# A fused Mamba, MLP and expert kernel: other priorities for the output norm's chain, earlier transposes, earlier statistics, and GpSimd's state products in front

## The chip, the cores and the metric

The kernel runs on one core of a Trainium2 chip. The metric is the device time of one execution in microseconds (us). Kernel before: 1598.88 us, median of three runs (1598.85 to 1601.64).

In the profile the engines are PE (TensorE, matrix products), PEld (its weight loads), DVE (VectorE), ACT (ScalarE), POOL (GpSimd) and SP (SyncE, which only issues DMAs here).

## The reference, cut to what matters

The input x has 2048 tokens of 512 float32 numbers.

```python
x = x + attn(layernorm(x))           # a Mamba-2 layer and a gated MLP
x = x + experts(layernorm(x))        # 8 experts, the best 2 of each token

def attn(r):
    h = r + mamba2(rmsnorm(r, ln1_w))
    return h + (silu(rmsnorm(h, ln2_w) @ gate_w) * (rmsnorm(h, ln2_w) @ up_w)) @ down_w

def mamba2(x):
    z, xb, B, C, dt = split(x @ in_proj_w)
    xb, B, C = split(silu(causal_conv(concat(xb, B, C))))      # 4 taps
    y = ssd_chunked(xb * dt, dt * A, B, C) + D * xb            # chunks of 128 tokens, a carried state
    y = rmsnorm(y * silu(z), norm_w)                           # the output norm
    return y @ out_proj_w
```

Between two chunks a state is carried: each chunk adds its own contribution to the decayed state, and reads the state before it.

## The kernel before, in words

**Tiling.** Tokens are cut into 16 chunks of 128 (t = 0 to 15). Two chunks form a block (b = 0 to 7; t = 2b and 2b + 1); four chunks form a block of the MLP (fb = 0 to 3). Everything is float32.

**A block b of the Mamba part.** `prepare(b)` makes the layer norm's statistics (`scales`: L144 and L145 give `mv`, L189 and L190 `rboth`), the normed tokens `hn` (L214), their transposes on PE (`transposed`, L196, into `pt`, copied to `hT` with the norm's weight at L200), `rstd` (L139, L140) and the step sizes. `project` makes the convolved channels: products `pm` (L332), a copy to `pre` on ACT (L344), two small copies on GpSimd (`halo`, L345 and L346), eight operations `ca` on DVE (L351, L353), a silu on ACT (L359) into `xb` or `cs`. `gate` makes `pz` on PE and its silu `zs` (L365). `chunk(t)` is a generator; in its order it yields: `ec` times `cs` on GpSimd (L401, for each half gp; it carries the old state's part), the scores `psc` (L406), exponentials (L412), their products `cum` on DVE (L414), `xd` (L420), `py` with the old state (L431) and with the scores (L439), the new state `pst` (L446), `yd` and `y` (L452, L455), the state (L461, L462) and its copies `sdiag` (L467); `xbt` (L381); the squares of y (`sq`, L475 and L476) and their sums on GpSimd (L478); the output product `po` (L483); and then **the output norm's chain**: `pms` on PE (L486), `ry` (square root on ACT L139, reciprocal on DVE L140), `h` from `po` (L493), the residual on GpSimd (L494) and its DMA issued from ACT (L495), the square sum of h (L498), `r2` (L139, L140), h times r2 (L501). Its last part transposes h (L196, copied to `h2T` at L200). That last part is run later, by `finish(ninth)` in `mamba(b)`.

**The MLP.** `feed_forward(fb)` runs 16 steps c. A step has four groups of products into two PSUM banks, `x1` (called `px` in the profile) and `x2` (`py`; the line is L711 for both): copies of `x1` on ACT (L756, L763), additions on DVE (L738, L744, L770), silus (L739, L745), and at the end of a step L775 on DVE, which multiplies by `x1` and thereby empties it for the next step, and L776 on GpSimd. The result goes through `mlp_down` (`pd`, L695; added at L696). In fb = 0, GpSimd makes combinations of the weights (`mg`, L526 and L527; `ms`, L537 and L538), and ACT issues the DMAs that keep them in DRAM (`early`, L539; `late`, L540).

**Order.** The kernel is written in a tile language whose scheduler orders every engine's instructions at compile time, by priority. `tc.high_priority(n)` puts instructions n places in front of where the program text has them. `tc.issue_after(i)` makes an engine's instructions stand behind instruction i. From b = 2 (`BPF`, the first block beside which a feed-forward block runs) PE alone is in a manual schedule: its instructions stand in the order in which the text makes them. In that part `mamba(b)` is a generator whose pieces alternate with groups of `feed_forward` (through `advance`). [...]

**What holds buffers.** `po` and `py` share one PSUM buffer (tag "y" of pool `ps_y`), all transposes and small products share one (tag "tr"), `sq` and `xd` share one SBUF buffer, `h` and `hn` three.

**The places of the change.** The chain stands under `tc.high_priority(SOON)` with SOON = 100. `prepare(b + 1)` is begun in `mamba(b)` during its first chunk, and its statistics are issued after `behind`, which at that time is `xd` of that same chunk t = 2b. The transposes of h are made by this piece of `mamba`, for the chunk before (`ninth`):

```python
                next(pieces)
                next(halves, None)
                yield
                if n % 4 == 0:
                    finish(ninth)
                if more and n < 3:
                    next(coming)
```

Of the kernel before, what the change touches and what calls it, by code (L numbers as in the profile page):

```python
# [23 lines left out]
TB = 256  # L24
NCH = TB // P
NB = T // TB
FB = 512
NFB = T // FB
DFF = 2048
FH = FB // 2  # L30
FC = 128
# [18 lines left out]
def mamba_mlp_moe(ctx, tc, x, w_in, w_out, w_gu, w_down, par, wr, wg, wu, wd, out):  # L50
# [93 lines left out]
        nc.vector.bn_stats(out=st, in_=src)  # L144
        nc.vector.bn_aggr(out=dst, in_=st)  # L145

    AT_ONCE, SOON = 400, 100

    early = const.tile([P, 1], F32, name="early")
    nc.scalar.activation(early, eps, AF.Sqrt)  # L150
# [168 lines left out]
    def finish(steps):  # L319
        while True:  # L320
            try:
                next(steps)
            except StopIteration as end:
                return end.value
# [57 lines left out]
        return xbt  # L382

    xbts = {}
    summed = None

    def chunk(b, j, dt, ncum, dtdec, cd, cum, ec, xb, cs, zs):

        nonlocal summed, behind
        t = b * NCH + j  # L390
        tok = slice(j * P, (j + 1) * P)
        halves = [slice(half * HD, (half + 1) * HD) for half in range(2)]
        sdt = sdiag[t % 2]
        xbt = xbts.pop(t)
        y = zs[:, :, tok]

        for gp in range(2):

            if t:
                with tc.issue_after(summed):  # L400
                    nc.gpsimd.tensor_tensor(ec[:, gp], ec[:, gp], cs[gp][:, :, tok], ALU.mult)  # L401

            psc = ps_sg.tile([P, 2, 4, P], F32, name=f"psc{t}_{gp}", tag="sg")
            for half in range(2):
                rows = halves[half]
                nc.tensor.matmul(psc[:, half], xb[rows, 2 + gp, tok], cs[gp][rows, :, tok], start=True, stop=True)  # L406


            lt = cum[gp].rearrange("p (a i) q -> p a i q", a=2)
            turns = [(half, i, 8 * gp + 4 * half + i) for i in range(4) for half in range(2)]  # L410
            for half, i, h in turns:
                nc.scalar.activation(lt[:, half, i], lt[:, half, i], AF.Exp, bias=ncum[:, j, h : h + 1])  # L412
            for half, i, h in turns:
                nc.vector.scalar_tensor_tensor(  # L414
                    lt[:, half, i], lt[:, half, i], dt[:, j, h : h + 1], psc[:, half, i], ALU.mult, ALU.mult
                )
            if gp == 0 and t < NT - 1:

                xd = wa.tile([P, 4, 4, HD], F32, name=f"xd{t}", tag="xd", bufs=1)
                added = nc.vector.tensor_tensor(  # L420
                    xd, bc(xbt[:, 0], 2, 4),
                    bc(dtdec[:, j, :].rearrange("p (g i) -> p g i", g=4), 3, HD), ALU.mult,
                )
                if t:
                    behind = added.ins
            if gp:
                yield
            py = ps_y.tile([P, 4, P], F32, name=f"py{t}_{gp}", tag="y")
            if t:
                for i in range(4):  # L430
                    nc.tensor.matmul(  # L431
                        py[:, i, :], sdt[:, gp, i, :], ec[:, gp, i, :], start=(i == 0), stop=False,
                        skip_group_check=True,
                    )
            yield
            if gp == 0:
                yield
            for half in range(2):
                nc.tensor.matmul(  # L439
                    py[halves[half]], xbt[:, 0, 2 * gp + half, :], lt[:, half], start=not t, stop=True,  # L440
                    skip_group_check=True,
                )
            if gp == 0 and t < NT - 1:
                pst = ps_tr.tile([P, 2, 4, HD], F32, name=f"pst{t}", tag="tr")
                for g in range(4):
                    nc.tensor.matmul(pst[halves[g % 2], g // 2], xbt[:, 1, g, :], xd[:, g], start=True, stop=True)  # L446


            yd = wa.tile([P, 4, P], F32, name=f"yd{t}_{gp}", tag="y")
            for i in range(4):  # L450
                at = C_D + 4 * gp + i
                nc.vector.scalar_tensor_tensor(  # L452
                    yd[:, i, :], xb[:, gp, tok], params[:, at : at + 1], py[:, i, :], ALU.mult, ALU.add
                )
            nc.vector.tensor_tensor(y[:, 4 * gp : 4 * gp + 4, :], yd, y[:, 4 * gp : 4 * gp + 4, :], ALU.mult)  # L455

        if t < NT - 1:
            new = state
            if t:
                flat = state.rearrange("p g i d -> p (g i) d")  # L460
                nc.gpsimd.tensor_tensor(flat, flat, bc(cd[:, j].rearrange("p g i -> p (g i)"), 2, HD), ALU.mult)  # L461
                nc.vector.tensor_tensor(state, state, pst, ALU.add)  # L462
            else:
                nc.vector.tensor_copy(state, pst)
            nxt = sdiag[(t + 1) % 2]
            for half in range(2):
                nc.scalar.copy(nxt[halves[half], :, :, half * HD : (half + 1) * HD], new[halves[half]])  # L467

        yield
        if t < NT - 1:  # L470
            xbts[t + 1] = turned_x(t + 1, xb if j == 0 else xc[0])

        sq = wa.tile([P, 8, P], F32, name=f"sq{t}", tag="xd", bufs=1)
        with tc.high_priority(AT_ONCE):
            nc.scalar.activation(sq[:, 0:4, :], y[:, 0:4, :], AF.Square)  # L475
            nc.scalar.activation(sq[:, 4:8, :], y[:, 4:8, :], AF.Square)  # L476
            for n in (4, 2, 1):
                summed = nc.gpsimd.tensor_tensor(sq[:, 0:n, :], sq[:, 0:n, :], sq[:, n : 2 * n, :], ALU.add).ins  # L478
        yield

        po = ps_y.tile([P, D], F32, name=f"po{t}", tag="y")
        for m in range(8):
            nc.tensor.matmul(po, y[:, m, :], w_o[:, m, :], start=(m == 0), stop=(m == 7))  # L483
        yield
        pms = ps_tr.tile([P, 1], F32, name=f"pms{t}", tag="tr")
        nc.tensor.matmul(pms, sq[:, 0, :], ones[:, 0:1], start=True, stop=True)  # L486

        with tc.high_priority(SOON):
            ry = wa.tile([P, 1], F32, name=f"ry{t}", tag="ry")
            rsqrt_eps(ry, pms, scale=1.0 / DI)  # L490
            h = wa.tile([P, D], F32, name=f"h{t}", tag="tok", bufs=3)
            nc.vector.tensor_scalar(h, res[t], mv[:, t, 0:1], rstd[:, t : t + 1], ALU.subtract, ALU.mult)
            nc.vector.scalar_tensor_tensor(h, po, ry, h, ALU.mult, ALU.add)  # L493
            nc.gpsimd.tensor_tensor(res[t], res[t], h, ALU.add)  # L494
            nc.scalar.dma_start(out=resd[t], in_=res[t])  # L495

            m2 = wa.tile([P, 1], F32, name=f"m2{t}", tag="m2")
            nc.scalar.activation(sq[:, 4:8, :].rearrange("p a q -> p (a q)"), h, AF.Square, accum_out=m2)  # L498
            r2 = wa.tile([P, 1], F32, name=f"r2{t}", tag="r2")
            rsqrt_eps(r2, m2, scale=1.0 / D)  # L500
            nc.vector.tensor_scalar_mul(h, h, r2)  # L501
        yield
        fb, off = divmod(t * P, FB)
        if off == 0:
            h2T[fb] = (wk if fb % 2 else wa).tile([P, 2, NK, FH], F32, name=f"h2T{fb}", tag="h2T", bufs=1)
        half, off = divmod(off, FH)
        transposed(h, h2T[fb][:, half, :, off : off + P], params[:, C_L2 : C_L2 + NK])
# [313 lines left out]
    def mamba(b):  # L821
# [12 lines left out]
        for j in range(NCH):  # L834
            pieces = chunk(b, j, dt, ncum, dtdec, cd, *near[j], xb, cs, zs)
            for _ in range(4):

                if n < 2:
                    halves = (gate(b, pair, hT, zs) for pair in (2 * n, 2 * n + 1))
                elif more:  # L840
                    halves = project(b + 1, n - 2, next_hT, *xc)
                else:
                    halves = iter(())
                next(pieces)
                if more and n == 0:
                    next(coming)
                if more and n == 3:
                    next(coming)
                if b == 0:
                    weigh(1)  # L850
                yield
                next(pieces)
                next(halves, None)
                yield
                if n % 4 == 0:
                    finish(ninth)
                if more and n < 3:
                    next(coming)
                elif more and n == 3:
                    ready = finish(coming)  # L860
                next(halves, None)
                if b == 0:
                    weigh(2)
                yield
                if more and n == 0:
                    next_hT = next(coming)
                yield
                n += 1
# [3 lines left out]
            if more:  # L872
                near[j] = spread(b + 1, j, ready[-1])

    BPF = FB // TB
    ninth = iter(())
    flow = []
    tail = iter(())
# [310 lines left out]
```

## Time and profile before

| | |
|---|---|
| median of three runs | 1598.88 us |
| the profiled execution | 1597.42 us |
| its span, first to last instruction | 1595.7 us |
| mean granted TensorE clock | 0.989 |
| PE busy | 1543.7 us |
| DVE busy | 770.5 us |
| ACT busy | 741.4 us |
| POOL busy | 399.9 us |

The profile is of one execution on the chip. A line of the timeline gives the start in us from the span's beginning, the duration, the engine, the line of the kernel, the operation, output and inputs, sizes, the number of instructions, and in square brackets the idle time of the engine before it and who ended it. The releaser is inferred from semaphores, and can be another one that used the same semaphore. A product in float32 is recorded twice, so "x4" of `px` is a group of two. Line numbers are those of the kernel before. Times by stage in the profile: the Mamba blocks alone up to about 214 us, Mamba beside the MLP from there to about 1093 us (the first group of MLP block 3 starts then), and after it the rest of the MLP and the experts.

### The profile page before, as it was taken

How to read it: one execution, taken by the hardware profiler on the slowest of the kernel's cores; microseconds unless marked ns; L12 is line 12 of the kernel's file. 1: busy time of each engine (PE TensorE's matmuls, PEld its weight loads, DVE VectorE, ACT ScalarE, POOL GpSimd, SP SyncE). 2: the span in 40 equal slices, each digit the busy share in tenths (PEclk: the TensorE clock that was granted, in tenths of full speed). 3: DMA queues.
4: the chain of work that ended last, by engine and by line, in shares of the span. 5: the costliest groups of instructions: out<-in, count | busy, mean ns of one | idle time of the engine just before them, and what ended most of it. 6: DMA issues, size and time to landing. Idle time of an engine off the chain costs nothing. (4 is left out here: it accounts for less than half of the span.)

```text
span 1595.7 us, 19155 instructions
## 1 busy us (share of the span) xinstructions
PE 1543.7 (97%) x6308; PEld 1051.4 (66%) x6308; DVE 770.5 (48%) x2018; ACT 741.4 (46%) x1335; POOL 399.9 (25%) x510
## 2 busy tenths in 40 slices
PE   9999888999999999999999999999999999999997
PEld 7556566767666777767676677666777666665563
DVE  7586854554455554645564654434354452221221
ACT  6788776666563775547645543222211221111110
POOL 2533324423242212111212111111011122333331
PEclk9899999999999999999999999999999999999999
DMA  9344434544553543334444522227777333333332
GB/s 316 117 128 136 154 110 162 182 142 147 170 192 132 190 155 113 127 125 138 129 142 160 175 93 86 92 99 265 256 228 228 103 68 58 67 66 67 66 67 33
DMA packets 127456, 218.68 MB, mean 137 GB/s; under 512 B 11584, under 2 KB 71488, under 8 KB 127360
## 3 DMA queue, kind: packets, MB, share of 16 engines
q1 hardware_dynamic: 105088, 166.08, 32.5%
q0 software_dynamic: 8736, 20.45, 7.0%
q10 hardware_dynamic: 13536, 30.94, 5.4%
q8 instruction: 52, 0.85, 0.2%
q14 instruction: 44, 0.36, 0.1%
HBM read 176.01 MB, written 41.42 MB: 136 GB/s over the span
## 5 line engine op out<-in xcount | busy, mean ns | idle before, releaser
L695 PE MATMUL pd<-md,a 128*128 128x512 f32 x512 | 238.5, 593 | 0.0
L332 PE MATMUL pm<-hT,wi 128*128 128x256 f32 x768 | 183.3, 384 | 1.3 <-DVE r L696 0.9
L696 DVE TENSOR_TENSOR r<-r,pd 128x512 f32<-128x512 f32 x128 | 87.6, 684 | 149.1 <-PE pd L695 148.0
L332 PEld LDWEIGHTS pm<-hT,wi 128*128 128x128 f32 x768 | 140.7, 190 | 26.2 <-issue 8.8
L695 PEld LDWEIGHTS pd<-md,a 128*128 128x128 f32 x512 | 97.0, 190 | 74.7 <-issue 66.5
L353 DVE SCALAR_TENSOR_TENSOR ca<-pre,params,ca 128x256 f32<-128x256 f32 x288 | 141.2, 543 | 0.3
L711 PE MATMUL py<-h2T,ms 128*128 128x256 f32 x512 | 132.1, 380 | 0.9 <-ACT up L750 0.7
L776 POOL TENSOR_TENSOR a<-a,up 128x256 f32<-128x256 f32 x64 | 47.8, 748 | 315.1 <-DVE up L770 246.1
L332 PE MATMUL pz<-hT,wi 128*128 128x256 f32 x512 | 123.3, 394 | 0.6 <-DMA wi<-in_w_in 0.6
L1045 PE MATMUL epg<-ew,xgT 128*128 x312 | 118.1, 460 | 0.4 <-issue 0.2
L1045 PE MATMUL epu<-ew,xgT 128*128 x312 | 117.8, 459 | 0.0
L483 PE MATMUL po<-w_o,zs 128*128 128x512 f32 x256 | 112.9, 592 | 0.0
L332 PEld LDWEIGHTS pz<-hT,wi 128*128 128x128 f32 x512 | 98.9, 198 | 19.8 <-issue 4.6
L1066 PE MATMUL epd<-ew,ehT 128*128 (+1 forms) x234 | 107.1, 593 | 1.0 <-DVE ehT L1059 1.0
L412 ACT ACT_TABLE_LOAD x71 | 91.1, 1283 | 34.3 <-DVE ncum L280 28.8
L711 PEld LDWEIGHTS py<-h2T,ms 128*128 128x128 f32 x512 | 95.0, 190 | 18.0 <-DVE a L744 2.4
L412 ACT ACTIVATE cum<-cum,ncum 128x128 f32<-128x128 f32 x256 | 87.1, 394 | 14.7 <-POOL cum L306 12.3
L483 PEld LDWEIGHTS po<-w_o,zs 128*128 128x128 f32 x256 | 48.3, 190 | 55.5 <-issue 54.0
L1026 POOL DMA_INDIRECT xg<-xnd,idx x39 | 38.8, 994 | 176.0 <-PE pt L196 174.0
L1045 PEld LDWEIGHTS epu<-ew,xgT 128*128 128x128 f32 x312 | 59.3, 190 | 33.0
L1072 POOL DMA_INDIRECT out<-ey,idx x39 | 61.9, 1587 | 66.8 <-DVE ey L1071 40.8
L711 PE MATMUL px<-h2T,mg 128*128 128x256 f32 x256 | 68.0, 388 | 10.7 <-DVE a L775 9.9
(248 smaller groups left out, 2504.5 us busy)
## 6 DMA issues: line engine op xcount, KB each, us to landing
wi<-in_w_in SPq DMA_DIRECT2D x80, 512.0 KB, 3.7
ms<-late SPq DMA_DIRECT2D x48, 512.0 KB, 3.7
mg<-early SPq DMA_DIRECT2D x48, 384.0 KB, 3.0
md<-in_w_down SPq DMA_DIRECT2D x64, 256.0 KB, 4.0
cum<-rowsd SPq DMA_DIRECT2D x32, 512.0 KB, 4.6
late<-ms ACTq DMA_DIRECT2D x16, 512.0 KB, 3.1
ec<-rowsd SPq DMA_DIRECT2D x60, 128.0 KB, 3.8
xnd<-xn ACTq DMA_DIRECT2D x28, 256.0 KB, 3.7
```

Source lines behind the costliest of these rows:

```text
L332: nc.tensor.matmul(pm[:, m, :], w[:, k, m * P : (m + 1) * P], hT[:, k, :], start=(k == 0), stop=(k == NK - 1))
L353: nc.vector.scalar_tensor_tensor(ca, pre[:, m, k : k + TB], cw[:, k : k + 1], ca, ALU.mult, ALU.add)
L412: nc.scalar.activation(lt[:, half, i], lt[:, half, i], AF.Exp, bias=ncum[:, j, h : h + 1])
L483: nc.tensor.matmul(po, y[:, m, :], w_o[:, m, :], start=(m == 0), stop=(m == 7))
L695: nc.tensor.matmul(pd, a[:, j * P : (j + 1) * P], d, start=(m == 0), stop=(m == 1))
L696: nc.vector.tensor_tensor(rows[j], rows[j], pd, ALU.add)
L711: nc.tensor.matmul(ps, w[:, k], m[:, k], start=(first and k == 0), stop=(k == KH - 1), skip_group_check=True)
L776: nc.gpsimd.tensor_tensor(a[:, 1], a[:, 1], up, ALU.mult)
L1026: nc.gpsimd.indirect_dma_start(out=xg, out_offset=None, in_=src, in_offset=bass.IndirectOffsetOnAxis(ap=idx[:, n : n + 1], axis=0))
L1045: nc.tensor.matmul(ps, xT[:, k, :], w[:, lo : lo + EI], start=(k == 0), stop=(k == NK - 1))
L1066: nc.tensor.matmul(pd, hT[:n, m, :], w[:n, NG + m * D : NG + (m + 1) * D], start=(m == 0), stop=(m == len(ET) - 1))
L1072: nc.gpsimd.indirect_dma_start(out=out, out_offset=bass.IndirectOffsetOnAxis(ap=idx[:, n : n + 1], axis=0), in_=y, in_offset=None, compute ...
```

## The change

Five edits, in the core of the diff:

```diff
-    AT_ONCE, SOON = 400, 100
+    AT_ONCE = 400
...
+    newest_xd = None
...
             if t:
-                with tc.issue_after(summed):
+                with tc.issue_after(summed), tc.high_priority(AT_ONCE):
                     nc.gpsimd.tensor_tensor(ec[:, gp], ec[:, gp], cs[gp][:, :, tok], ALU.mult)
...
-                if t:
-                    behind = added.ins
+                behind, newest_xd = newest_xd or behind, added.ins
...
-        with tc.high_priority(SOON):
+        with tc.high_priority(AT_ONCE if t == BPF * NCH - 1 else 0):
             ry = wa.tile([P, 1], F32, name=f"ry{t}", tag="ry")
             rsqrt_eps(ry, pms, scale=1.0 / DI)
...
                 next(pieces)
+                if n % 4 == 0 and (b != BPF or n):
+                    finish(ninth)
                 next(halves, None)
                 yield
-                if n % 4 == 0:
+                if b == BPF and n == 0:
                     finish(ninth)
```

- The chain of the output norm has a priority of 400 at t = 3 (`BPF * NCH - 1`), and none at the other fifteen chunks, where it had 100 at all sixteen.
- The transposes of h are made one piece sooner in the text, ahead of half a projection (`halves`) and of one group of the MLP, at every turn but b = 2, n = 0 (the chunk t = 3).
- The statistics of a block are issued behind `xd` of the chunk before the one that they stood behind.
- GpSimd's product `ec` times `cs` has a priority of 400.
- No instruction is computed with other operands than before; nothing is added to or left out of the computation.

## The prediction, on record before the result was known

> **What bounds the kernel now.** First the page's busy times:
>
> ```profile
> PE 1543.7 (97%) x6308; PEld 1051.4 (66%) x6308; DVE 770.5 (48%) x2018; ACT 741.4 (46%) x1335; POOL 399.9 (25%) x510
> ```
>
> TensorE (PE) is the bound: 97% busy, no other engine over half. From b = 2 on its order is the one written in the program, so a moved instruction elsewhere is worth only what it takes off (or adds to) PE's idle time, plus what a slower PE clock costs. So next the waits of PE, longest first in total (columns: waited for, us in total, times, longest us):
>
> ```profile
> PE px L711 <- DVE a L775: 9.9, 7, 1.8
> PE py L431 <- POOL halo L346: 7.5, 2, 5.0
> PE pt L196 <- DVE hn L214: 4.8, 2, 3.7
> PE pt L196 <- DVE h2T L200: 3.1, 4, 0.8
> ...
> PE pt L196 <- DVE mv L145: 1.5, 1, 1.5
> ```
>
> These five are 26.8 us, and all lie in the stages that the change touches. The timeline of PE around the largest (start us, duration us, last the idle time before it):
>
> ```profile
> 195.21 2.05 PE L431 MATMUL py<-ec,sdiag 128*128 128x128 f32 x8 [4.98 <-POOL halo L346]
> ...
> 203.27 0.63 PE L196 MATMUL pt<-ident,h 128*128 128x128 f32 x4 [1.51 <-DVE mv L145]
> 207.63 1.09 PE L196 MATMUL pt<-ident,hn 128*128 128x128 f32 x4 [3.73 <-DVE hn L214]
> 208.51 5.79 PE L332 MATMUL pz<-hT,wi 128*128 128x256 f32 x16
> ```
>
> The first releaser is misnamed. GpSimd's product `ec` (L401) had ended at 188.47, its `halo` copy at 194.73; but `py` shares its only buffer (tag "y") with `po`, and DVE's L493, which empties `po`, ended at 195.11, 0.10 before PE went on. At 117.36 it is the same (L493 ends 117.26). So these two stalls wait for the output norm's chain, not for GpSimd. And sixteen pz records take 5.79 us here against 3.6 us at 347.8. The table of windows tells why (PE busy, PEld, DVE, ACT, POOL, then PEclk):
>
> ```profile
> 117.30:120.70 3.40, 3.34 (x12) 3.10 (x13) 3.40 (x8) 2.61 (x6) 1.30 (x1) 0.50 0.21 80
> 195.20:199.20 4.00, 3.99 (x14) 3.55 (x15) 4.00 (x9) 3.20 (x6) 1.30 (x1) 0.50 0.42 164
> 206.10:212.90 6.80, 5.27 (x15) 4.40 (x16) 4.34 (x7) 4.55 (x7) 2.51 (x2) 0.50 0.01 2
> ```
>
> [...] the granted clock is 0.50 after each of the long waits. [...] L353 took 0.98 each at 185.8 (2.95 for 3) beside a busy GpSimd, 0.41 at 196.6 (2.45 for 6) beside an idle one. [...]
>
> **The change, part by part**, in the built order of each engine.
>
> *A. t = 3: its norm in front, the statistics of b = 3 a chunk sooner.* Before, ACT stood from 189.30 to 192.45 behind two DMA issues (`early`, `late`, released by GpSimd's 192.06), then loaded a table and made `ry` at 194.01. After, the load, `rboth` and `ry` come ahead of those issues: 189.3 + 1.28 + 0.3 + 0.3 = 191.2. But DVE now has six operations on `ca_10`, `ca_11` ahead of its reciprocal of `ry`, beside GpSimd's five products: from 188.9, four at 0.98, two at 0.5 give 193.8; the reciprocal 0.16, one more `ca` 0.5 to 1.0, L493 0.74: 195.2 to 195.8. So the 4.98 us gap stays, or grows by up to 0.6; I take 0.6. Only if the `ca` operations ran at 0.41 would L493 end near 193.0. Then: `cum` x8 2.2, `hn` 0.55, `xd` 1.2, `hn` 0.55, r and h 0.8: h is there at about 201.9, while PE reaches its transposes at 195.8 + 2.0 + 4.7 = 202.5: the 1.51 goes. `hn` is ready, so the 3.73 goes; next late is the single "tr" buffer, 0.78 as at t = 5. Hence `pt<-hn` starts at 202.5 + 0.6 + 0.8 = 203.9 instead of 207.6: 3.7. With no long gap, the half clock of 206.1 to 212.9 doesn't come: its 5.3 busy us shrink by half, 2.6. Sum 6.3; bounds 2.5 (contended throughout) and 9 (the first gap shrinks to 3 as well).
>
> *B. t = 1, the same turn at 117.36.* `ry` comes 1.4 sooner on ACT (one load less ahead), but six `ca` operations (two at 0.37, four at 0.5: 2.8) again precede it on DVE: 112.5 + 2.8 + 0.16 + 0.5 + 0.74 = 116.7 against 117.26. Gain 0.3 after what the transposes lose; bounds -1.5 and 2.2 (a half-clock window more or less).
>
> *C. The chain's priority goes from 100 to 0 for t other than 3.* At t = 4 to 7, PE waits for `a` L775, which empties `x1`. Timeline of ACT, then of DVE, at t = 4:
>
> ```profile
> 266.40 1.28 ACT L139 ACT_TABLE_LOAD   x1
> ...
> 268.01 1.28 ACT L739 ACT_TABLE_LOAD   x1
> 269.30 0.42 ACT L739 ACTIVATE a<-a 128x256 f32<-128x256 f32 x1
> ```
> ```profile
> 270.30 0.49 DVE L501 TENSOR_SCALAR h<-h,r 128x512 f32<-128x512 f32 x1
> 270.70 0.41 DVE L775 TENSOR_TENSOR a<-a,px 128x256 f32<-128x256 f32 x1
> ```
>
> The norm's square root (two loads and 0.3) stands ahead of the silu, and its scaling ahead of L775. After, silu comes first: 266.40 + 0.42 = 266.8 with no load; L775 comes right behind `xd` (ends 267.71), 268.1; `pd` keeps PE busy until 269.39. So the whole gap goes, and likewise at 340.40, 422.64 and 491.74: 1.78 + 1.76 + 1.78 + 1.62 = 6.9. Bounds 5 and 6.9. What is later is h: at t = 4 271.4 instead of 270.8.
>
> *D. Transposes a piece sooner.* At t = 5, 7, 9, 11 `pt<-h` is directly followed by `pt<-hn`, one buffer, 4 x 0.78 = 3.1 waiting for `h2T`. After, 8 pz, 2 px, 2 py lie between (12 products of two records, 24 x 0.216 = 5.2 us): 3.1 goes. The cover: h was ready 11 to 15 us before its transposes at t = 4 to 13, and 5.7 to 9.8 before their new place, so the 0.6 of part C is hidden. At t = 12 `pt<-h` now follows `pt<-xn` and waits some 0.65 for ACT's copy (ends 881.13), but that covers the 0.87 that `pm` waited there: +0.2. At t = 14 it moves by six matmuls, over 4 us of slack left.
>
> *E. GpSimd's products for the state in front.* They end no stall. What they push back: at c = 5 and 13 of the first feed-forward block, `ec` (L401) now precedes `ms` (L538). In the timeline of GpSimd, then of ACT:
>
> ```profile
> 315.03 0.72 POOL L538 TENSOR_TENSOR ms<-ms,mg 128x256 f32<-128x256 f32 x1
> 315.71 1.27 POOL L401 TENSOR_TENSOR ec<-ec,cs 128x512 f32<-128x512 f32 x1
> ```
> ```profile
> 315.79 0.33 ACTq L540 DMA_DIRECT2D late<-ms  x1
> 316.14 1.28 ACT L739 ACT_TABLE_LOAD   x1 [1.06 <-POOL ms L538]
> ```
> ACT's issue of `late` waits for `ms`; the silu's load and silu queue behind it; L775 (ends 318.30) behind the silu; PE's next `px` started at 318.36, 0.06 later, so with no slack (469.77 and 469.82 at c = 13). A 1.27 us product in front becomes a new PE wait of 1.27, twice: -2.5. Bounds -2.6 and 0. At c = 1 the same swap (one add of `sq`, 1.2) holds `xbt` about 0.5, and PE waits for it at 243.40: -0.5. Moved statistics put `rboth` and two `hn` before L775 at c = 3 and 11: 285.8 against 286.8 wanted, hidden by 1.0. SP's moved loads (four, `wi` and `x`) meet no PE wait.
>
> Sum: 6.3 + 0.3 + 6.9 + 3.1 + 0.2 - 2.5 - 0.5 = 13.8. The profiled execution took 1597.42 (span 1595.7 and 1.7 around it): 1583.6. The median shown, 1598.88, is 1.46 above it: 1585.1. I say 1585.
>
> **Rivals.** (1) A gives nothing beyond its idle time, or less: [...] B loses 1.5, and hidden steps of c = 3 and 11 surface at 1 us each: 13.8 - 3.8 - 1.8 - 2 = 6.2, about 1592.7. For it: the first gap stays, and 2.12 us of waiting at 45.3 already brought 10.2 us at 0.50. (2) Slower: the chain without priority misses its earlier transposes, in which case PE, in order, waits at each of ten of them (t = 4 to 13). To end 3.2 above before it must eat 13.8 + 3.2 = 17, so 1.7 at each, h late by 7.4 to 11.5: 1602. Against it: part C's 0.6. (3) Nothing moves: what looks like PE's gain is taken by the next of its waits (248.28, 1.70; 234.01, 0.51, both left alone) and by `late` more often than twice: within 0.2% (3.2 us), 1597.
>
> **Numbers.** Forecast (gain 7 to 20) 0.80, rival 1 0.10, rival 2 0.05, rival 3 0.05. 0.2%, 3.2 us, is about what a measurement of this kernel tells from no change. Faster 0.90, same 0.05, slower 0.05. Range: A at 9 (+2.7), B at 2.2 (+1.9) and no loss at c = 1 (+0.5) make 18.9, with 1 for the spread of the runs 1579; A at 2.5 (-3.8), B at -1.5 (-1.8), C at 5 (-1.9) and 0.5 more in E leave 5.8, so 1593, beyond which lie rivals 2 and 3 and an edge of the others.
>
> **What would show it.** Right: no wait of `px` for `a` at t = 4 to 7; none of `pt` for `h2T` at t = 5 to 11, and one of 0.8 at t = 3; none for `hn`; the half clock after 206 gone; two new waits of 1.2 to 1.3 for L775's line at c = 5 and 13; the gap ahead of `py` at t = 3 still 4 to 6. Wrong: PE waiting for `h` at an early transpose, or a first gap under 3.

## The result, and the profile after

| | before | after |
|---|---|---|
| median | 1598.87 us (4 runs, 1598.45 to 1601.64) | 1587.80 us (4 runs, 1586.32 to 1587.97) |
| the profiled execution | 1597.42 us | 1587.97 us |
| its span | 1595.7 us | 1586.0 us |

The ratio is 0.9925, with a 95% interval from 0.9908 to 0.9942: faster by 11.1 us in the medians and by 9.4 in the profiled executions, against 13.8 forecast. The time is 2.8 above the number that was forecast and inside its range (1579 to 1593). Line numbers of the kernel after are one to three higher than before (L711 is now L713, L775 is L777, L431 is L432, L144 is L145).

The page's busy times after; PE is busy for 0.7 us less, so 9.0 of the 9.7 us that the span lost are idle time of PE:

```profile
PE 1543.0 (97%) x6308; PEld 1051.8 (66%) x6308; DVE 768.4 (48%) x2018; ACT 722.7 (46%) x1321; POOL 403.7 (25%) x510
```

The longest waits of PE after (waited for, us in total, times, longest us):

```profile
PE py L432 <- issue: 6.8, 2, 5.4
PE px L713 <- DVE a L777: 6.7, 5, 3.1
PE pc L269 <- ACT xbt L382: 2.6, 2, 1.4
...
PE pt L197 <- DVE h2T L201: 0.8, 1, 0.8
```

The waits for `hn` and for `mv` are gone from the top, those for `h2T` fell from four to one. But the wait of `px` for L777 fell by only 3.2 us, and its longest is now 3.1 where none was over 1.8. The timeline of PE around t = 3 is as the prediction has it: the first gap is still there (0.4 longer), no wait for `hn`, 0.79 for the buffer:

```profile
197.93 2.04 PE L432 MATMUL py<-ec,sdiag 128*128 128x128 f32 x8 [5.37 <-issue]
199.77 5.43 PE L333 MATMUL pz<-hT,wi 128*128 128x256 f32 x16
205.03 0.60 PE L197 MATMUL pt<-ident,h 128*128 128x128 f32 x4
206.42 0.66 PE L197 MATMUL pt<-ident,hn 128*128 128x128 f32 x4 [0.79 <-DVE h2T L201]
206.91 3.40 PE L333 MATMUL pz<-hT,wi 128*128 128x256 f32 x15
```

The table of windows (after the stretch: PE busy, PEld, DVE, ACT, POOL, then PEclk) shows that the half clock after 206 is gone, and that a new stretch has come at 719:

```profile
206.10:212.90 6.80, 6.48 (x34) 5.46 (x36) 4.53 (x9) 4.47 (x6) 2.77 (x2) 1.00 0.87 291
718.90:722.10 3.20, 3.20 (x8) 2.57 (x9) 3.20 (x11) 0.95 (x3) 0.19 (x1) 0.50 0.00 0
```

What happened at 719? First PE's timeline, then DVE's, of the kernel after:

```profile
714.67 1.16 PE L432 MATMUL py<-ec,sdiag 128*128 128x128 f32 x8
718.90 2.07 PE L713 MATMUL px<-h2T,mg 128*128 128x256 f32 x4 [3.07 <-DVE a L777]
```
```profile
708.63 1.23 DVE L422 TENSOR_TENSOR xd<-xbt,dtdec 128x1024 f32<-128x1024 f32 x1 [1.06 <-ACT sq L500]
709.77 0.69 DVE L145 BATCH_NORM_STATS2 bn<-x 128x6 f32<-128x512 f32 x1
...
712.16 0.49 DVE L503 TENSOR_SCALAR h<-h,r 128x512 f32<-128x512 f32 x1
715.42 0.69 DVE L145 BATCH_NORM_STATS2 bn<-x 128x6 f32<-128x512 f32 x1 [2.77 <-DMA x<-in_x]
716.03 0.17 DVE L290 TENSOR_TENSOR dtdec<-dtdec,dt 128x32 f32<-128x32 f32 x1
716.12 0.68 DVE L698 TENSOR_TENSOR r<-r,pd 128x512 f32<-128x512 f32 x1
716.72 0.61 DVE L352 TENSOR_SCALAR ca<-pre,params 128x256 f32<-128x256 f32 x2
717.25 1.27 DVE L354 SCALAR_TENSOR_TENSOR ca<-pre,params,ca 128x256 f32<-128x256 f32 x3
718.43 0.41 DVE L777 TENSOR_TENSOR a<-a,px 128x256 f32<-128x256 f32 x1
```

The first of the two moved statistics (709.77) finds its tile. The second waits 2.77 us for the load of x15, and everything behind it on DVE waits with it (nothing runs there from 712.65 to 715.42), L777 last. Why does x15 come so late? The pool of x tiles has five buffers, so x15 takes that of x10, and x10 is in use until its residual has been written. In order, from POOL, ACT's queue and SP's queue, and last what SP waited for from 700 to 716 (us, times, longest):

```profile
706.07 1.27 POOL L496 TENSOR_TENSOR x<-x,h 128x512 f32<-128x512 f32 x1 [11.62 <-DVE h L495]
```
```profile
707.37 0.33 ACTq L497 DMA_DIRECT2D resd<-x  x1
```
```profile
711.89 0.33 SPq L79 DMA_DIRECT2D x<-in_x  x1
```
```profile
SPq L79 <- DMA resd<-x: 2.2, 1, 2.2
```

The write is issued at 707.37, SP waits for it, the load is issued at 711.89, and the statistic can start 3.5 later. The answer on the load's line says who waited for it (us in total, times):

```profile
  DVE bn L145: 10.8, 6
```

One of the six is the start of the kernel, which every kernel here has (2.5 to 2.8); the other five, 8.2 us, came with the moved statistics, for b = 2 and 4 to 7.

To see what each costs, the start of the same group of PE was subtracted between two timelines (kernel less before, us; a change between two rows is gained or lost between them):

| PE's start, us in before | before | after | after, again | no_ec | stats_old | bufs6_md3 | b3_exact |
|---|---|---|---|---|---|---|---|
| first `pms`, 76.65 | 0 | 0.4 | 0.1 | 2.2 | 1.5 | 0.9 | -2.2 |
| `psc` of t = 4, 189.10 | 0 | 2.3 | 2.0 | 4.2 | 1.4 | 1.8 | -3.0 |
| first `px`, 214.57 | 0 | -3.8 | -4.6 | -1.8 | 1.6 | -5.0 | -9.7 |
| first `px` of fb = 1, 522.59 | 0 | -11.0 | -12.1 | -11.8 | -5.8 | -6.5 | -17.2 |
| `pst` of t = 10, 666.65 | 0 | -12.3 | -13.4 | -12.6 | -7.1 | -7.8 | -18.4 |
| `px` at 728.71 | 0 | -9.8 | -11.1 | -10.7 | -7.1 | -7.7 | -18.4 |
| `pst` of t = 12, 817.58 | 0 | -9.4 | -10.7 | -10.6 | -8.3 | -9.0 | -19.7 |
| end | 0 | -9.7 | -10.8 | -10.8 | -8.2 | -3.8 | -19.9 |

All these kernels give PE the same instructions between the first rows, though not in the same order. After loses 1.9 us between the first two rows, where among other things the second statistic of b = 2 waits (1.18 at 88.89), and 2.8 between t = 10 and t = 12, where other kernels gain 1.3.

### The profile page after: what moved, and what is told of

Read it like the earlier page. It is cut to its first block, busy times and chain, and to the rows that moved or that the text cites. A ratio compares the mean times of both kernels' runs of the same rounds, so it can differ in the third digit from the quotient of the medians.

```text
span 1586.0 us, 19153 instructions
## 1 busy us (share of the span) xinstructions
PE 1543.0 (97%) x6308; PEld 1051.8 (66%) x6308; DVE 768.4 (48%) x2018; ACT 722.7 (46%) x1321; POOL 403.7 (25%) x510
## 5 line engine op out<-in xcount | busy, mean ns | idle before, releaser
L713 PE MATMUL py<-h2T,ms 128*128 128x256 f32 x512 | 132.1, 380 | 0.9 <-ACT up L752 0.7
L713 PEld LDWEIGHTS py<-h2T,ms 128*128 128x128 f32 x512 | 94.9, 190 | 18.1 <-DVE a L746 2.4
L199 ACT COPY xgT<-pt 128x512 f32<-128x512 f32 x39 | 22.8, 586 | 117.7 <-PE pt L197 117.7
```

The lines of the kernel that those rows point to most:

```text
L713: nc.tensor.matmul(ps, w[:, k], m[:, k], start=(first and k == 0), stop=(k == KH - 1), skip_group_check=True)
```

## The experiments

Theory: A, C and D do what the prediction says, E costs its two waits, and the shortfall is DVE's wait for x tiles. Rival: the shortfall is something else (the priorities, the statistics' own work in a new place, an accident of the clock). The runs were made on three chips, each beside the kernel before, whose medians there were 1599.22 (experiments 1 and 2, stats_b3, and 4), 1597.98 (5, 6 and b3_noec_front) and 1599.21 (b3_exact, front_exact and 8).

**1. GpSimd's product back in its place (no_ec).**

```diff
-                with tc.issue_after(summed), tc.high_priority(AT_ONCE):
+                with tc.issue_after(summed):
                     nc.gpsimd.tensor_tensor(ec[:, gp], ec[:, gp], cs[gp][:, :, tok], ALU.mult)
```

> The changed kernel without its GpSimd edit: the product ec (L403) keeps the planner's place behind ms. Theory (step E): the two new waits of px for L777 at c = 5 and 13 (1.09 and 1.08 us) go and nothing else moves, so 2.2 us below the changed kernel: about 1585.6. Rival (the products in front also bring something, at c = 1 or ahead of py): the waits go, but others of about the same size come back, and the time stays within 0.5 us of 1587.8, or rises.

Measured: 1585.54 us, ratio 0.9910 (0.9896 to 0.9923). In the kernel after, PE waits here at c = 5 (timeline of PE):

```profile
314.13 1.13 PE L713 MATMUL px<-h2T,mg 128*128 128x256 f32 x4 [1.09 <-DVE a L777]
```

and in no_ec the same group starts with no wait:

```profile
312.84 1.88 PE L697 MATMUL pd<-md,a 128*128 128x512 f32 x4
314.57 1.13 PE L713 MATMUL px<-h2T,mg 128*128 128x256 f32 x4
```

Over the first MLP block (rows 3 and 4 of the table) no_ec gains 10.0 where after gains 7.2. So the edit on GpSimd costs 2.8 us and brings nothing that could be seen. By the starts of `px`, each of the two waits costs 1.2; the other 0.3 or so lies around c = 3. The stall at 719 stays (2.53).

**2. Statistics as before (stats_old).**

```diff
-                behind, newest_xd = newest_xd or behind, added.ins
+                if t:
+                    behind = added.ins
```

> The changed kernel with the statistics pinned as before for every b; the other edits stay. Theory: the waits for x tiles go (prologue 2.3, stall at 719 3.8), but at t = 3 the wait for hn (3.73) and the half-clock window after it (2.6) return: 6.1 - 6.3 = about no difference, 1587 to 1589. Rival (the shortfall comes of something else): the loss of A's 6.3 with nothing back, 1594.

Measured: 1589.34 us, 0.9936 (0.9921 to 0.9950). Rows 1 to 2: no loss. Rows 5 to 7: a gain of 1.3 for the loss of 2.8. But between `psc` of t = 4 and the first `px` the gain of 6.1 is gone as well, with the wait for `hn` back (PE's waits):

```profile
PE pt L197 <- DVE hn L215: 4.1, 2, 3.7
```

So the statistics, moved for every b, bring 6.3 and cost 2.0 and 4.1: little on balance (the ratio of 0.9936 is that of the changed kernel within the interval, 0.9925 and in experiment 8 0.9935). What the 2.0 consist of is told under B below.

**3. Statistics sooner for b = 3 alone (stats_b3), and a mend of it (b3_exact).**

```diff
-                behind, newest_xd = newest_xd or behind, added.ins
+                behind, newest_xd = newest_xd if b == BPF else added.ins, added.ins
```

> The changed kernel with the statistics a chunk sooner for b = 3 alone (those that step A needs at t = 3); for every other b they stand where they stood before. Theory (the missed step: the second statistic waits on VectorE for an x tile whose buffer is freed only just ahead): of 10.8 us that VectorE waited for x tiles only the one of b = 3 stays, if any; the loss of 2.3 us ahead of t = 1 and the wait of 3.07 us with its half clock at 719 go, and A's gain stays: 6 us below the changed kernel, 1582 (1581 to 1584). Rival (the shortfall against the forecast comes of something else[...]): within 1 us of 1587.8.

Measured: 1585.08 us, 0.9912 (0.9898 to 0.9926). The waits for x tiles fell to the first (2.7 us, once), the stall at 719 is 0.79. It is above the 1581 to 1584 that were expected. The expectation says too much: at t = 0 the line moves the statistics of b = 1 back by a chunk as well, and the prologue took another order: its first `pms` is 6.0 later than in the kernel before, where after is 0.4 and no_ec 2.2 later. At t = 3 the other order was a gain: the gap ahead of `py` is 0.76, with 3.93 waited later for `h2T`. A mend leaves b = 1 alone:

```diff
+                if t:
+                    behind = newest_xd if b == BPF else added.ins
+                newest_xd = added.ins
```

> The kernel with statistics sooner for b = 3 alone had moved those of b = 1 as well (a chunk later, since at t = 0 nothing may move), and its prologue took 4 us more. Here b = 1 too stands as before, so that against the changed kernel only the statistics of b = 2 and 4 to 7 differ. Theory: from the end of the prologue to t = 2 the loss of 2.1 us against the kernel before falls to 0.3 or less, A stays at -6.1 with its gap of 5.4 ahead of py, and from t = 10 to t = 12 the loss of 2.8 turns into a gain of 1.3 as in the kernels without early statistics there: 5 to 6 below the changed kernel of the same chip, about 1582.5. Rival (the repair before gained from the other order of the prologue and t = 3 alone): 1586 or more.

Measured: 1583.21 us, 0.9906 (0.9892 to 0.9921), 4.8 below the changed kernel on the same chip (1587.97, experiment 8), where each of its runs (to 1584.18) is below each run of that (from 1584.46). Its built order is that of stats_old but for the stage of t = 3. From rows 1 to 2 it gains 0.8, from rows 2 to 3 6.8, from rows 5 to 7 1.3. (Its profile is of its lowest run, 5.5 below its median, so the last row of the table flatters it.) PE and DVE at the place of the stall:

```profile
710.31 1.13 PE L715 MATMUL px<-h2T,mg 128*128 128x256 f32 x4 [0.79 <-DVE a L779]
```
```profile
708.65 1.27 DVE L354 SCALAR_TENSOR_TENSOR ca<-pre,params,ca 128x256 f32<-128x256 f32 x3
709.84 0.41 DVE L779 TENSOR_TENSOR a<-a,px 128x256 f32<-128x256 f32 x1
```

The same group of `px` takes 1.13 us here and 2.07 after: the clock is whole (1.00 in the window 710.30 to 713.50, 0.50 in that after). So the wait for x15 cost 2.3 us of idle time more, and the stretch of about 3.4 us at half clock (an estimate from the clock of wider windows, 0.98 from 715 to 719 and 0.59 from 719 to 723: 4 x 0.02 and 4 x 0.41, over 0.5) some 1.7: together about the 4.1 of rows 5 to 7.

**4. A sixth buffer for x (bufs6_md3).** The statistics stay where the change put them.

```diff
-    xp = pa_stack.enter_context(tc.tile_pool(name="xp", bufs=5))
+    xp = pa_stack.enter_context(tc.tile_pool(name="xp", bufs=6))
...
-        d = pmlp.tile([P, D], F32, name="md", tag="md", bufs=4)
+        d = pmlp.tile([P, D], F32, name="md", tag="md", bufs=3)
```

> The changed kernel with the pool of x tiles at six buffers for five, the room for it taken from the down projection's weights (three buffers for four). Statistics stay a chunk sooner everywhere. Theory (it is the late buffer, not the earlier place of the statistics): VectorE waits for no x tile, and the prologue's loss and the stall at 719 go: 4 to 6 us below the changed kernel, 1582 to 1584, less what later loads of the down weights may cost. Rival (the statistics' own work, 0.6 us for each tile and 0.55 for each hn, stands in VectorE's way in its new place): no wait for x tiles, but the time within 1 us of 1587.8.

Measured: 1593.95 us, 0.9968 (0.9957 to 0.9979): slower than after. The theory's part held and the price of the buffer was far underrated. Waits for x tiles: the first only (2.8). Between the first two rows 0.9 lost instead of 1.9, at 719 nothing, rows 5 to 7 a gain of 1.3. So it is the late tile, not the statistics' own work, that stalls there; of the 1.9 ahead of t = 4 about half is the wait. Against that stand 13 waits for the down projection's weights, which have a buffer less (PE's waits):

```profile
PE pd L697 <- DMA md<-in_w_down: 8.0, 13, 1.6
```

**5. The priority alone (prio_only), the earlier transposes alone (trans_only),** each made in the kernel before:

```diff
-    AT_ONCE, SOON = 400, 100
+    AT_ONCE = 400
+    BPF = FB // TB
...
-        with tc.high_priority(SOON):
+        with tc.high_priority(AT_ONCE if t == BPF * NCH - 1 else 0):
```

> The kernel before with the priority edit alone: the norm's chain in front at t = 3, no priority at all other t. Theory (step C is the priority's alone): the four waits of px for L775's line at t = 4 to 7 (1.78, 1.76, 1.78, 1.62) go, the waits of pt for h2T at t = 5, 7, 9, 11 and for hn at t = 3 stay, no wait for x tiles beyond the one there was: 6.9 below the kernel before, give or take 1 at t = 1 and 3: 1592. Rival (C needs the earlier transposes or statistics too): fewer than two of the four waits go, above 1596.

Measured: 1589.48 us, 0.9955 (0.9943 to 0.9967), 8.5 below before, where 6.9 were expected. The four waits at t = 4 to 7 are gone, the rest is there (PE's waits):

```profile
PE pt L197 <- DVE hn L215: 4.1, 2, 3.7
PE pt L197 <- DVE h2T L201: 3.1, 4, 0.8
PE px L712 <- DVE a L776: 2.9, 3, 1.6
```

Over the first MLP block it gains 8.0, by four steps of 1.9 to 2.0 each.

```diff
                 next(pieces)
+                if n % 4 == 0 and (b != FB // TB or n):
+                    finish(ninth)
                 next(halves, None)
                 yield
-                if n % 4 == 0:
+                if b == FB // TB and n == 0:
                     finish(ninth)
```

> The kernel before with the earlier transposes alone. Theory (step D): the four waits of pt for h2T (0.78 each) go and the four of px for L775's line stay: 3.1 below before, 1596. Rival (with the chain's priority still 100 nothing else moves, but h comes too late for the earlier place): PE waits for h at its transposes, and the time does not fall.

Measured: 1593.33 us, 0.9973 (0.9962 to 0.9983), 4.7 below before, where 3.1 were expected. No wait for `h2T` is left, and the waits of `px` are all there (10.1 us, 7). Between the first `px` and that of fb = 2 it gains 4.3, 1.0 to 1.3 at each of the four places.

**6. Two repairs together (b3_noec):** stats_b3 and no_ec.

> Two repairs of the changed kernel at once: statistics a chunk sooner for b = 3 alone, and the GpSimd product ec in the planner's place as before. Theory: the two add up, since they lie in different stages. From the profile with the statistics alone (end 14.98 us below the kernel before) another 2.3 for the two waits at L777 (1.09 and 1.30 there): a profile 17 below, a median of 1582.5. Rival (the spread of the prologue hides it, or ec in its old place brings another wait back): no lower than 1585.

Measured: 1582.49 us, 0.9908 (0.9894 to 0.9922), as expected, but the medians alone don't show that the two add up: the ratios of stats_b3 and no_ec are 0.9912 and 0.9910, within the interval. Nor is the profile 17 below before, but 14.6, since its first `pms` is 7.8 later. The stages show it: from the first `px` to the end after gains 5.9, no_ec 9.0, stats_b3 9.6 and this one 12.4. What they bring alone, 3.1 and 3.7, is 6.5 together.

**7. And the front at t = 3 (b3_noec_front; with the mend of 3, front_exact).**

```diff
+                with tc.high_priority(AT_ONCE if b == BPF + 1 else 0):
-                nc.vector.tensor_scalar(
-                    hns[j], res[t], mv[:, t, 0:1], rboth[:, t : t + 1], ALU.subtract, ALU.mult
-                )
+                    nc.vector.tensor_scalar(
+                        hns[j], res[t], mv[:, t, 0:1], rboth[:, t : t + 1], ALU.subtract, ALU.mult
+                    )
...
-        transposed(h, h2T[fb][:, half, :, off : off + P], params[:, C_L2 : C_L2 + NK])
+        with tc.high_priority(AT_ONCE if t == BPF * NCH - 1 else 0):
+            transposed(h, h2T[fb][:, half, :, off : off + P], params[:, C_L2 : C_L2 + NK])
```

> The same two repairs, and at t = 3 the transposes' eviction into h2T and the two hn of b = 3 get the front priority as well. With the repaired statistics alone PE waited 3.93 us there for h2T (L201), which stood on VectorE behind eight products of cum, an xd and an hn. Theory: in the built order h2T now stands behind five products of cum and hn is made ahead of the convolution, so the wait falls to about 0.8 (one buffer of tag tr), while the wait of py ahead of it grows by 0 to 0.5: 2.6 to 3.1 below the kernel with two repairs, about 1579.7. Rival (the wait only moves on, to xd or to the next product): no lower than it by more than 1.

Measured: 1579.56 us, 0.9882 (0.9868 to 0.9895). The 2.9 (against b3_noec on the same chip) came, with other parts than expected: the wait for `h2T` is 1.65, that of `py` 1.92, and sixteen records of `pz` take 3.62 us there (5.43 after), so the clock stays whole.

> The kernel with two repairs and the front priority at t = 3, with the statistics of b = 1 back in their place. Theory: the prologue gets its 4 us back, but in the built order the reciprocal of ry stands behind five operations on ca again, so the gap ahead of py at t = 3 is 5.4 and not 1.9, and what follows in that stage is no better: about the same time, 1578 to 1581. Rival (the prologue's length does not depend on that order): 1583.

Measured: 1579.47 us, 0.9884 (0.9867 to 0.9900), as expected: the first `pms` comes 8.1 sooner than in b3_noec_front, but at the first `px` only 0.3 of it is left. 3.1 are lost between, and 4.7 at t = 3, where the gap ahead of `py` is 5.37 again. Both are about 8.3 us below the changed kernel, and beat both kernels; they cannot be told apart.

**8. The changed kernel again (after_again).**

> The changed kernel itself once more, beside the two others on one chip. Theory: 1587.8 within 1.5; the waits for x tiles at about the same places and sizes (10.8 in all), PE's wait of some 3 us at 719 again, while the waits before 80 us differ from run to run[...]. Rival (the stall at 719 was of that one execution): no wait over 1 us there.

Measured: 1587.97 us, 0.9935 (0.9919 to 0.9951). Waits for x tiles 10.4 us, 6 times; the stall at 719 is 2.93. It belongs to the kernel.

## Why the prediction was right or wrong

Measured by the table of starts, each part in the run named; "t = 12" is what was forecast under D for the transposes there.

| step | forecast | measured | from |
|---|---|---|---|
| A, t = 3 | 6.3 | 6.1 | after, rows 2 to 3 |
| B, t = 1, and the rest of rows 1 to 2 | 0.3 | -1.9 | after, rows 1 to 2 |
| C, priority | 6.9 | 8.0 | prio_only |
| D, transposes | 3.1 | 4.3 | trans_only |
| t = 12 | 0.2 | 0.2 | trans_only |
| E, GpSimd in front | -3.0 | -2.8 | no_ec against after |
| second statistics wait at t = 10 and 11 | 0 | -4.1 | after against b3_exact |

The measured parts add up to 9.8, against 9.7 of the span. That the number came so close was in part luck: B and the last row took 6.3 more than forecast, and C and D gave 2.3 more, for which the prediction had no reason. B's -1.9 and C's 8.0 lie outside the bounds that were given for them.

**A** came as worked out: the 4.98 became 5.37 (forecast 5.58), the wait of 0.79 for the buffer took the place of 3.73, and the second half clock went (1.00 from 206.10 to 212.90). That the priority at t = 3 doesn't bring A by itself is shown by stats_old and prio_only, both with 3.73 for `hn`; whether the earlier statistics would bring it without the priority, no run shows. (The prediction's sum for h being there gives 201.1, not 201.9, which changes nothing, since PE was expected at 202.5.)

**C** and **D** were right in place and count, and short in size by 0.2 to 0.5 us a wait. The idle time that the records showed was not the whole cost: waits of 1.62 to 1.78 cost 1.9 to 2.0 (prio_only), waits of 0.78 cost 1.0 to 1.3 (trans_only). Where PE didn't wait, the records of two groups overlapped by 0.15 to 0.2 us (in the kernel after `pz` starts at 199.77 while `py` lasts to 199.97; in no_ec `px` starts at 314.57 while `pd` lasts to 314.72); after a wait that overlap is missing (in the kernel after `px` starts at 314.13, 1.09 behind the end of `pd` at 313.04). By the author's estimate this accounts for about 0.2 of each; the rest of D's is open.

**E** was right: two waits of 1.09 and 1.08 (forecast 1.27). By the starts they cost 1.24 and 1.22. The 0.5 at c = 1 didn't show: the wait for `xbt` grew from 0.57 to 1.45, and the next one of `px` fell from 1.70 to 0.92, but in no_ec they are 1.40 and 0.91 as well, so this isn't the work of the edit on GpSimd.

**B**'s own stage gained more than forecast. Its gap shrank from 2.49 to 1.46, and no half clock follows it (1.00 from 116 to 128): between the starts at 112.25 and 122.12 of before, after gains 2.7. Two losses outweigh this. Ahead of it, from 76.65 to 112.25, the late x tile delays PE by 1.6 (0.3 in bufs6_md3). Behind it, from 122.12 to 144.99, the four profiled kernels with the statistics of all blocks moved (after, after_again, no_ec, bufs6_md3) lose 2.7 each, where stats_old, prio_only and b3_exact lose 0 to 0.7 (stats_b3 loses 3.4, by waits of PE, 2.09 for `dA` the longest). This loss is in no term of the prediction. It comes of PE's order, which is the scheduler's before b = 2, and which changed with the statistics. PE's timeline of before, then of after:

```profile
126.11 1.08 PE L439 MATMUL py<-cum,xbt 128*64 128x512 f32 x4
127.11 1.13 PE L406 MATMUL psc<-cs,xb 64*128 64x512 f32 x4
```
```profile
125.89 1.07 PE L440 MATMUL py<-cum,xbt 128*64 128x512 f32 x2
126.89 0.66 PE L197 MATMUL pt<-ident,hn 128*128 128x128 f32 x4
127.48 1.07 PE L440 MATMUL py<-cum,xbt 128*64 128x512 f32 x2
128.48 1.12 PE L408 MATMUL psc<-cs,xb 64*128 64x512 f32 x2
129.53 1.08 PE L447 MATMUL pst<-xd,xbt 128*64 128x256 f32 x8
130.55 1.12 PE L408 MATMUL psc<-cs,xb 64*128 64x512 f32 x2
```

Four records in a row take as long as two (1.13 and 1.12 for `psc`, 1.08 and 1.07 for `py`): in before two records of `psc` run at once (both in the window 127.10 to 127.60), in after one (128.48 to 128.95). With the transposes of `hn` and with `pst` between them the pairs take 1.07 and 1.12 each, one after the other: about 1.0 lost twice. The other 0.7 is a longer wait for `dA` (0.94 at 147.01, for 0.25).

The stall at t = 10 isn't in the sum either. The other step that failed is one sentence under E: "Moved statistics put `rboth` and two `hn` before L775 at c = 3 and 11: 285.8 against 286.8 wanted, hidden by 1.0. SP's moved loads (four, `wi` and `x`) meet no PE wait." It counted the time of the moved instructions in the first MLP block, and took their input for granted. What it left out is when that input can be there: the second x tile of block b takes the buffer of chunk 2b - 4, whose residual is written at the beginning of chunk 2b - 3. The statistics stood behind `xd` of chunk 2b - 2; now they stand behind that of 2b - 3, and the tile lands 1 to 3 us after they could start. The waits of b = 4, 5 and 6 (1.83, 1.24, 1.17 on DVE) cost PE nothing that the table shows, so part of the sentence held. Those of b = 2 and 7 surfaced: for b = 2 as about 1.0 (the 1.9 of after less the 0.9 of bufs6_md3), for b = 7 as 4.1. In fb = 1 the statement was never tried.

**The rivals.** Rival 1 named the right kind of thing (hidden steps that surface), at the wrong places and 4.9 too slow. The slower rival didn't come: after t = 3 no transposes of `h` wait but those of t = 12, 0.68 us for ACT's copy (0.65 forecast), where `pm` no longer waits its 0.87. And not every loss was needed: with the statistics moved for b = 3 alone, and without the edit on GpSimd, the change is worth 15.5 us (b3_noec, which also has b = 1 a chunk later), and 18 to 20 with the front at t = 3.

## What to carry to other kernels

When a consumer moves forward, look for its inputs before its costs: for each buffer it reads, follow the pool back to who frees it, and compare the landing of the load in the trace of before with the new place. Here one early statistic became a wait for all that stood behind it on DVE (2.77 us at 715.42, and through L777 3.07 on PE); so move such an instruction only where the early place is needed (here one block of seven), and leave the others. And where a scheduler makes the order, compare the order of the bottleneck engine as well: here it parted products whose records had run two at a time, at about 1.0 us for each of the two pairs.

## What the runs showed of the hardware that was not expected

**A half clock may cost little.** In the kernels before and after, a wait of about 2.1 us at 45 (2.12 and 2.15) was followed by some 10 us at half clock (0.50 from 45.60 to 55.90 in before, and from 46.40 to 56.40 in after; a wider window of after: PE busy, PEld, DVE, ACT, POOL, PEclk):

```profile
48.00:58.00 10.00, 10.00 (x29) 6.11 (x28) 3.17 (x10) 5.60 (x13) 7.51 (x6) 0.57 0.11 39
```

In no_ec, with the same built order on PE, the clock stayed whole (1.00 from 44 to 66), and PE then waited instead (timeline of PE):

```profile
68.70 0.38 PE L269 MATMUL pc<-tri,dA 128*32 128x128 f32 x2 [4.81 <-DVE dA L266]
```

At the first `pms` it was 1.8 later than after. In this execution PE at whole clock arrived early and waited for DVE. Not every run is like that: b3_exact had the whole clock as well (1.00 from 44 to 66), waited 1.58 there, and was 2.6 sooner than after. So these runs show no cost of that stretch beyond the spread of the prologue, and not that it has none. That its cost hangs on whether the other engines wait for PE there is the author's guess, and no run tests it.

**Which wait is followed by the half clock isn't told by its length.** Behind waits of 1.96 (prio_only) and 2.15 us (after) at 45 the clock was 0.52 and 0.57 from 48 to 58; waits of 1.82 to 2.17 there in four others (b3_exact, no_ec, bufs6_md3, stats_old) left it at 1.00 until 58. So one wait of 1.96 was followed by it in one execution and one of 2.17 was not in another. In the kernel before, the clock of 0.50 followed the waits of 2.12 (45.60 to 55.90), 2.49 (117.30 to 120.70) and 4.98 (195.20 to 199.20), and was there from 206.10 to 212.90, around the end of that of 3.73 (207.63). What the prediction says of the long waits holds for that trace; a length from which it would hold elsewhere was not shown.

**The prologue's length differs from run to run by 2 to 4 us** at the same order of PE's instructions: 0.1, 0.4 and 2.2 in the table's first row for after_again, after and no_ec, and 1.5 against -2.2 for stats_old and b3_exact, which differ only from t = 3 on. The runs of b3_exact go from 1577.66 to 1584.18, and its profiled one is the lowest. Differences under 2 us were therefore read from single stages and not from medians.
